# Layer 0 attention's beginning: the first four heads' parts sent ahead, zero fills on ScalarE, other batches' norms placed behind the first scores

## The chip, the cores and the metric

The kernel runs on one core of a Trainium2 chip. The metric is the device time of one launch in microseconds (us); the time before is the median of three runs.

The core's engines have queues of their own, and each works through its queue in order: TensorE (PE, with its weight loads as PEld), VectorE (DVE), ScalarE (ACT), GpSimd (POOL) and SyncE (SP), which here only issues transfers (DMA). An instruction that waits holds everything behind it on its engine.

## The reference, cut to what matters

A decoder of four layers runs on x of shape 4 x 512 x 128 (batches, tokens, width). Each layer is an attention, a cross-attention to a context of 77 rows, and a feed-forward with experts, each added to x. The change is in the first of these twelve parts, and touches the second:

```
x = x + L0_attn(layernorm(x), W_attn, b_attn, W_proj, b_proj, temperature)
x = x + L0_xattn(ctx, ctx, layernorm(x), ...)
```

`L0_attn` has 16 heads of width 8. Its scores are q k^T / sqrt(8) divided by a temperature, with a bias for the distance of two tokens (a slope for each head), and a causal mask; softmax and the product with v follow, then a projection with W_proj. The kernel keeps the accuracy of 32 bits in the scores by splitting q and k into three bf16 parts each and multiplying the parts.

## The kernel before, in words

The program is written for a planner (the Tile framework): Python code emits instructions in one order; the planner puts each on its engine's queue, may move an instruction ahead of earlier ones that are not ready by its own account, and adds the waits. `weave(dense, chain, every)` (L386) interleaves two generators when emitting: after `every` steps of the first it takes one of the second. What the planner makes of it is seen in the trace.

At the start `Net.__init__` fetches x of batch 0, weights, constants and x of batches 1 to 3 (L318, L371), and makes the identity, the ones and the causal mask on GpSimd. `norm(0)` (L491) follows: statistics of four tiles of 128 tokens (L479, L480), a reciprocal square root by Newton steps on 128x4 elements (L465 to L470), scaling on ScalarE (L487), four TensorE transposes into the PSUM tile s, of which there is one (L511), and a copy to xT (L512).

`l0_attn` (L1034) then prepares its tiles. The two tiles `vs` (one batch each, alternating; 128 x 2048 elements) are filled with zeros, and every ninth column of a group of 32 with ones, on GpSimd (L1057, L1058). `project(b)` makes a batch's q and k: two matmuls of xT (L421), q on VectorE (L1089), k on ScalarE (L1090); the parts, by casts on ScalarE (L1094, L1098) and subtractions on VectorE (L432), into `q3` and `k5`; a copy of two parts of `k5` on GpSimd (L1101), so that three consecutive parts can be taken in three rotations. Then the parts are written to DRAM, one transfer for q (L1105) and three for k (L1107), in all for 16 heads at once; last come the values v (L1112, L1113). `load(b, g)` brings the rows of four heads (group g) from DRAM into `qs[g]` and `ks[g]` in six transfers of 96 KB (L1121, L1122), in which a row of the contraction is a partition.

`rounds(first, last)` runs 16 items (4 batches x 4 groups). For item 0, `project(0)`, `load(0, 0)`, the bias row (L1076) and `load(0, 1)` come first. In a round the scores of one item are computed in 11 units (L1132, the mask added by L1135), each followed by a maximum on VectorE (L1139); beside them stand the scores again, transposed and less the maxima, with the exponential, of the item before (L1177 to L1185), whose maxima are sent as rows into `qs` (L1161 to L1165), and the product with v of the item before that (L1199). The next batch's `project` is spread over the round of its predecessor's second group, and each round loads the item two ahead.

At the end, the caller weaves rounds 0 to 6 with a chain: `norm(1)`, `norm(2)`, `norm(3)` and `l0_context`, which projects the 77 context rows of the four batches for the cross-attention (matmuls L421 on tile s, a copy L427, an addition L1315, a copy L429). One step of the chain is emitted after four steps of the rounds.

Of the kernel before, what the change touches and what calls it, by code (L numbers as in the profile page):

```python
# [14 lines left out]
BF16 = mybir.dt.bfloat16  # L15
# [7 lines left out]
P = 128  # L23
B, S, D = 4, 512, 128
NT = B * S // P
TB = S // P
# [12 lines left out]
class Pack:  # L39


    def __init__(self):
        self.parts, self.at, self.n = [], {}, 0
# [246 lines left out]
class Net:  # L290
# [7 lines left out]
    def __init__(self, ctx, tc, packs, dram, feed):  # L298
        self.tc, self.nc = tc, tc.nc
        self.packs, self.dram = packs, dram  # L300
        self.feed, self.loaded = feed, []
        self.stay = {}
        self.turn = 0
        self.last = []
        self.chunks, self.sums = {}, {}
        nc = self.nc
        pool = lambda name, bufs, **kw: ctx.enter_context(tc.tile_pool(name=name, bufs=bufs, **kw))
        self.keep = pool("keep", 1)
        self.wpool = pool("weights", self.SLOTS)
        self.small = pool("small", 4)  # L310
        self.away = pool("away", 1, space=bass.MemoryType.DRAM)

        k = self.keep
        self.x = k.tile([P, NT, D], F32, name="x")
        self.xn = k.tile([P, NT, D], F32, name="xn")
        self.xT = k.tile([P, NT * P], F32, name="xT")
        xin = dram["x"].rearrange("(t p) d -> p t d", p=P)
        fetch = lambda b: nc.sync.dma_start(self.x[:, TB * b : TB * b + TB, :], xin[:, TB * b : TB * b + TB, :])  # L318
        fetch(0)
        self.want(0)  # L320
        self.const = self.load("const", k, "const")
        self.want(1)
        for b in range(1, B):
            fetch(b)
        self.ident = k.tile([P, P], F32, name="ident")
        make_identity(nc, self.ident)
        self.ones = k.tile([P, P], F32, name="ones")
        nc.gpsimd.memset(self.ones, 1.0)
        self.identb = k.tile([P, P], BF16, name="identb")
        nc.vector.tensor_copy(self.identb, self.ident)  # L330

        self.causal = k.tile([P, P], BF16, name="causal")
        nc.gpsimd.memset(self.causal, 0.0)
        nc.gpsimd.affine_select(
            out=self.causal, in_=self.causal, pattern=[[-1, P]], compare_op=ALU.is_ge,
            fill=-BIG, base=0, channel_multiplier=1,
        )
# [3 lines left out]
    def pool(self, name, bufs=1, right=False):  # L341
        return self.tc.tile_pool(
            name=name, bufs=bufs, side="right" if right else "left", reuse_waits="tile"
        )
# [21 lines left out]
    def load(self, name, pool, tag, cols=None):  # L366
        at, n = self.packs[name]
        src = self.dram[name]
        t = pool.tile([P, cols or n], F32, tag=tag, name="w_" + name.replace(".", "_"))
        cast = src.dtype != F32  # L370
        (self.nc.gpsimd if cast else self.nc.sync).dma_start(t[:, :n], src)  # L371
        return Weights(t, at)
# [25 lines left out]
    def turns(self, *chains):  # L398

        chains = [iter(c) for c in chains]  # L400
        while chains:
            for c in list(chains):
                try:
                    yield next(c)
                except StopIteration:
                    chains.remove(c)

    def lagged(self, items, *phases):

        for r in range(len(items) + max(lag for _, lag in phases)):  # L410
            for phase, lag in phases:
                if 0 <= r - lag < len(items):
                    phase(*items[r - lag])
                    yield
# [619 lines left out]
    def l0_attn(self, pool, W, Wo):  # L1034
# [3 lines left out]
        nc, tc = self.nc, self.tc  # L1038
        one = lambda shape, name, dt=F32: pool.tile(shape, dt, name=name, bufs=1)
        K1, K2 = 81, 99  # L1040
        qs = [one([K2, 4, S], f"qs{g}", BF16) for g in range(4)]
        ks = [one([K2, 4, S], f"ks{g}", BF16) for g in range(4)]
# [11 lines left out]
        vs = [one([P, TB, 16, 32], f"v{i}") for i in range(2)]  # L1054
        for v in vs:

            nc.gpsimd.memset(v, 0.0)  # L1057
            nc.gpsimd.memset(v[:, :, :, 8:9], 1.0)  # L1058

        rows = one([48, 16], "own_rows")  # L1060
# [19 lines left out]
        made, ys, stacks = {}, {}, {}  # L1080

        def project(b):

            xb = self.tokens(b)
            pq, pk = self.mm(), self.mm()
            self.dot(pq, (W["wq"], xb))
            self.dot(pk, (W["wk"], xb))
            q, k = (pool.tile([P, S], F32, tag=n, name=n, bufs=1) for n in "qk")
            nc.vector.tensor_scalar(q, pq, W["bq"], sc, ALU.add, ALU.mult)  # L1089
            nc.scalar.activation(k, pk, AF.Identity, bias=W["bk"])  # L1090
            yield
            q3, k5 = pool.tile([P, 3, S], BF16, tag="q3", name="q3"), pool.tile([P, 5, S], BF16, tag="k5", name="k5")
            for a, out in ((q, q3), (k, k5)):
                nc.scalar.copy(out[:, 0], a)  # L1094
                self.tt(a, a, out[:, 0], ALU.subtract)
            yield
            for a, out in ((q, q3), (k, k5)):
                nc.scalar.copy(out[:, 1], a)  # L1098
                self.tt(out[:, 2], a, out[:, 1], ALU.subtract)
            yield  # L1100
            nc.gpsimd.tensor_copy(k5[:, 3:5], k5[:, 0:2])  # L1101
            qd = self.away.tile([16, 24, S], BF16, name=f"q_parts{b}")
            kd = [self.away.tile([16, 24, S], BF16, name=f"k_parts{b}_{c}") for c in range(3)]
            flat = lambda d: d.rearrange("h (d p) t -> (h d) (p t)", p=3)
            nc.sync.dma_start(flat(qd), q3.rearrange("r p t -> r (p t)"))  # L1105
            for c in range(3):
                nc.sync.dma_start(flat(kd[c]), k5[:, c : c + 3].rearrange("r p t -> r (p t)"))  # L1107
            stacks[b] = qd, kd
            yield
            ps = self.mm((P, TB, 16, 8))  # L1110
            for j in range(TB):
                self.dot(ps[:, j].rearrange("p h d -> p (h d)"), (self.tile_of(TB * b + j), W["wv"]))  # L1112
            nc.scalar.copy(vs[b % 2][:, :, :, :8], ps)  # L1113
            yield

        def load(b, g):

            qd, kd = stacks[b]
            for c in range(3):
                r = slice(24 * c, 24 * c + 24)  # L1120
                nc.sync.dma_start(qs[g][r], qd[4 * g : 4 * g + 4].rearrange("h r t -> r h t"))  # L1121
                nc.sync.dma_start(ks[g][r], kd[c][4 * g : 4 * g + 4].rearrange("h r t -> r h t"))  # L1122

        def score_units(b, g):

            m = made[b, g, "m"] = pool.tile([P, TB, 4], F32, tag="m", name="m", bufs=2)

            def unit(i, h0, per):
                n = (i + 1) * P
                ps = self.mm((P, per, n))  # L1130
                for h in range(per):
                    nc.tensor.matmul(  # L1132
                        ps[:, h], lhsT=qs[g][:K1, h0 + h, i * P : n], rhs=ks[g][:K1, h0 + h, :n], start=h == 0, stop=False
                    )
                nc.tensor.matmul(  # L1135
                    ps[:, :, i * P :], lhsT=self.identb, rhs=self.causal.unsqueeze(1).to_broadcast([P, per, P]),
                    start=False, stop=True,
                )
                nc.vector.tensor_reduce(m[:, i, h0 : h0 + per], ps, AX.X, ALU.max, negate=True)  # L1139

            return [
                lambda i=i, h0=h0, per=per: unit(i, h0, per)
                for i, per in ((3, 1), (2, 1), (1, 2), (0, 4)) for h0 in range(0, 4, per)
            ]
# [89 lines left out]
        def rounds(first, last):  # L1234
            n = len(items)
            item = lambda i: items[i] if 0 <= i < n else None
            if first == 0:
                yield from project(0)
                load(0, 0)
                biases()  # L1240
                load(0, 1)
                yield
# [927 lines left out]
def chained(*chains):  # L2170
    for c in chains:
        yield from c
# [10 lines left out]
def build(nc, packs, dram):  # L2183
# [11 lines left out]
    with tile.TileContext(nc) as tc, ExitStack() as ctx:  # L2195
        net = Net(ctx, tc, packs, dram, feed)
# [3 lines left out]
        def open_pool(name, right=False):  # L2200
            pools[name] = ExitStack()
            return pools[name].enter_context(net.pool(name, right=right))
# [10 lines left out]
        s1 = open_pool("s1", right=True)  # L2213
# [3 lines left out]
            pass  # L2217
        rounds = net.l0_attn(a0, *[net.pack(i, feed[i]) for i in range(2)])
        w1 = net.load("s1", s1, "w")
        net.weave(rounds(0, 7), chained(net.norm(1), net.norm(2), net.norm(3), net.l0_context(s1, w1)), 4)  # L2220
        net.want(at["l0a"] + 1)

        def chain1(group):
# [62 lines left out]
        rounds = net.l2_ffn(f2, gv, y, away, passes, where, wants)  # L2286
# [57 lines left out]
        chain = chained(net.norm(3), net.route_dense(3, W5, s5))  # L2344
# [31 lines left out]
```

## Time and profile before

| what | value |
|---|---|
| median of 3 runs | 2305.12 us (2304.5 to 2309.32) |
| the profiled execution's own time | 2308.67 us |
| its span | 2306.8 us |
| TensorE busy | 2164.1 us (94%) |
| VectorE busy | 1600.5 us (69%) |
| ScalarE busy | 1027.8 us (45%) |
| GpSimd busy | 556.6 us (24%) |
| first score matmul (L1132) starts | 33.2 us |
| moved by DMA in the whole span | 204.72 MB |

The span is what the profiler records between the first and the last instruction; the time of an execution is a little longer. Busy time is the time in which an engine executes; weight loads overlap matmuls. In a timeline a line gives start, length, engine, line of the code, operation, output<-input, size and count; in brackets, how long the engine had been idle before and what ended it. A count above one joins neighbouring instructions. "SPq" is SyncE's queue: its lines are transfers being issued, not their landing.

### The profile page before, as it was taken

The numbers are of one execution on the slowest core, as the hardware profiler recorded it, in microseconds if no ns is written. First come the engines' busy times: TensorE is split into PE (matmuls) and PEld (weight loads), VectorE is DVE, ScalarE is ACT, GpSimd is POOL, SyncE is SP. The second block draws the span as 40 slices with busy tenths as digits, with TensorE's granted clock in tenths as the row PEclk, the third lists the DMA queues.
The fourth block names the chain that finished last, engine by engine and source line by source line (L and its number), as shares of the span: only waits on it lengthen the run. The fifth ranks groups of instructions, "written<-read, shape, count | busy, mean of one in ns | idle before, by whom it ended". The sixth has DMA issues, their size and how long they took to land. (4 is left out here: it accounts for less than half of the span.)

```text
span 2306.8 us, 28326 instructions
## 1 busy us (share of the span) xinstructions
PE 2164.1 (94%) x9154; PEld 1142.8 (50%) x9154; DVE 1600.5 (69%) x4027; ACT 1027.8 (45%) x2102; POOL 556.6 (24%) x693
## 2 busy tenths in 40 slices
PE   6999899999999998999999999999999999498878
PEld 3566556554545553444444444444444444465553
DVE  6666576566675779777967696767776765686636
ACT  4555446444325462544444344444444444165432
POOL 1000001000000002333323333333333332335552
PEclk8988899999999999999999999999999999799779
DMA  6321134153453344233333344333333334200022
GB/s 165 99 61 43 45 108 132 51 141 104 110 148 90 90 103 117 59 94 94 92 85 82 87 113 108 103 103 94 103 103 94 82 99 101 92 1 6 1 71 75
DMA packets 81774, 204.72 MB, mean 89 GB/s; under 512 B 18799, under 2 KB 37551, under 8 KB 81371
## 3 DMA queue, kind: packets, MB, share of 16 engines
q1 hardware_dynamic: 78058, 198.99, 32.2%
q0 software_dynamic: 3568, 3.93, 0.6%
q8 instruction: 72, 1.18, 0.2%
q14 instruction: 76, 0.61, 0.1%
HBM read 173.94 MB, written 23.40 MB: 86 GB/s over the span
## 5 line engine op out<-in xcount | busy, mean ns | idle before, releaser
L1756 POOL TENSOR_TENSOR gvx<-gvx 128x512 f32<-128x512 f32 (+1 forms) x256 | 259.8, 1015 | 583.7 <-DVE gvx L432 528.6
L421 PE MATMUL f<-xT,w_l_ffn 128*128 128x512 f32 (+1 forms) x768 | 367.9, 601 | 1.2 <-ACT h L1001 0.7
L1876 ACT ACTIVATE at_e<-mm,at_m 128x512 f32<-128x512 f32 x256 | 172.8, 685 | 215.3 <-DVE at_m L1874 209.6
L421 PE MATMUL mm<-w_l_ffn_qkv,xT 128*128 128x512 f32 x512 | 265.5, 603 | 3.3 <-DVE roped L1727 1.7
L1845 PE MATMUL mm<-og,w_l_ffn_o 128*128 128x512 f32 x512 | 264.6, 600 | 0.0
L432 DVE TENSOR_TENSOR h<-h,f 128x512 f32<-128x512 f32 (+1 forms) x192 | 131.3, 685 | 136.1 <-PE f L421 110.3
L1001 ACT ACTIVATE h<-f 128x512 f32<-128x512 f32 x189 | 112.4, 596 | 249.7 <-PE f L421 217.2
L421 PEld LDWEIGHTS f<-xT,w_l_ffn 128*128 128x128 f32 (+1 forms) x768 | 139.5, 191 | 149.0 <-issue 126.1
L1009 PE MATMUL acc<-h,w_l_ffn 128*128 128x512 f32 x378 | 193.4, 596 | 3.5 <-DVE h L432 2.9
L432 DVE TENSOR_TENSOR og<-mm,c 128x512 f32<-128x512 f32 x256 | 175.8, 688 | 29.0 <-PE mm L1845 27.6
L432 DVE TENSOR_TENSOR gvx<-mm,gv 128x512 f32<-128x512 f32 x256 | 174.3, 683 | 23.6 <-PE mm L421 18.9
L1796 ACT COPY eT<-mm 128x512 f32<-128x512 f32 x256 | 137.5, 595 | 73.3 <-PE mm L1795 73.0
L1874 DVE TENSOR_REDUCE at_m<-mm 128x1 f32<-128x512 f32 x256 | 161.2, 683 | 8.9 <-PE mm L421 7.2
L1795 PEld LDWEIGHTS mm<-ident,at_e 128*128 128x128 f32 x1024 | 120.1, 141 | 67.0 <-issue 49.5
L1845 PEld LDWEIGHTS mm<-og,w_l_ffn_o 128*128 128x128 f32 x512 | 89.4, 191 | 97.0 <-issue 85.3
L1795 PE MATMUL mm<-ident,at_e 128*128 128x128 f32 x1024 | 134.1, 273 | 2.6 <-ACT at_e L1876 2.6
L421 PE MATMUL mm<-roped 64*128 64x512 f32 x512 | 133.4, 623 | 1.5 <-DVE roped L432 1.0
L421 PEld LDWEIGHTS mm<-w_l_ffn_qkv,xT 128*128 128x128 f32 x512 | 86.7, 190 | 91.9 <-issue 69.4
L1139 DVE TENSOR_REDUCE m<-mm 128x1 f32<-128x512 f32 (+3 forms) x176 | 105.3, 637 | 35.5 <-PE mm L1135 34.7
L1812 PE MATMUL mm<-eT,v 128*64 128x512 f32 x512 | 119.5, 599 | 0.0
L1009 PEld LDWEIGHTS acc<-h,w_l_ffn 128*128 128x128 f32 x378 | 70.9, 191 | 92.9 <-issue 66.9
L432 DVE TENSOR_TENSOR h<-h,c 128x512 f32<-128x512 f32 x160 | 111.1, 700 | 3.9 <-DMA c<-l_ffn_w 1.1
(457 smaller groups left out, 3646.3 us busy)
## 6 DMA issues: line engine op xcount, KB each, us to landing
c<-gates SPq DMA_DIRECT2D x256, 256.0 KB
c<-l_ffn_w SPq DMA_DIRECT2D x96, 384.0 KB
w_l_ffn<-in_l_ffn SPq DMA_DIRECT2D x26, 576.0 KB
w_l_ffn_qkv<-in_l_ffn_qkv SPq DMA_DIRECT2D x16, 640.0 KB
w_l_ffn_o<-in_l_ffn_o SPq DMA_DIRECT2D x16, 512.0 KB
rot<-qk SPq DMA_DIRECT2D x128, 64.0 KB
k_parts<-k SPq DMA_DIRECT2D x12, 384.0 KB
qs<-q_parts SPq DMA_DIRECT2D x48, 96.0 KB
```

Source lines behind the costliest of these rows:

```text
L421: self.nc.tensor.matmul(out, lhsT=lhsT, rhs=rhs, start=i == 0, stop=i == len(pairs) - 1)
L432: self.nc.vector.tensor_tensor(out, a, b, op)
L1001: nc.scalar.activation(h, pg, AF.Silu)
L1009: nc.tensor.matmul(acc["t"], lhsT=W["d" + u], rhs=h, start=i == 0, stop=i == n - 1)
L1139: nc.vector.tensor_reduce(m[:, i, h0 : h0 + per], ps, AX.X, ALU.max, negate=True)
L1756: nc.gpsimd.tensor_tensor(x[:, :, :m], x[:, :, :m], x[:, :, m : 2 * m], ALU.add)
L1795: nc.tensor.transpose(p[:, j, :], es[i][hl][:, j * P : j * P + P], self.ident)
L1796: nc.scalar.copy(eT[hl][:, :, i * P : i * P + P], p)
L1812: nc.tensor.matmul(po[64 * hl : 64 * hl + 64, :], lhsT=m["v"][:, j, hl, :], rhs=eT[hl][:, j, :], start=j == 0, stop=j == TB - 1,)
L1845: nc.tensor.matmul(acc, lhsT=W["o"][:, (e - 1) * D : e * D], rhs=hs.pop(e - 1), start=e == 1, stop=e == E)
L1874: nc.vector.tensor_reduce(m, s, AX.X, ALU.max, negate=True)
L1876: nc.scalar.activation(e[:, :n], s, AF.Exp, bias=m, accum_out=den)
```

## The change

Five edits, all in the first stage:

- the zero fills of `vs` move from GpSimd to ScalarE, as a scaled copy of the ones by 0.0;
- the copy of two parts of `k5` moves from GpSimd to VectorE, for every batch;
- batch 0's parts go to DRAM in two sets of four transfers, heads 0 to 3 and then heads 4 to 15, in DRAM tiles of their own; `load(b, g)` finds the tile that holds its group;
- `load(0, 0)` is emitted between these two sets instead of after `project(0)`;
- the chain of norms and context is wrapped in `after_scores`: once a first score matmul has been emitted, every TensorE instruction of the chain is ordered behind it on TensorE's queue (an order of issue, no wait for its end). Instructions of the chain on other engines are not ordered by it.

```diff
+    def after_scores(self, chain):
+
+        while True:
+            with ExitStack() as order:
+                if self.first_score:
+                    order.enter_context(self.tc.issue_after(self.first_score.ins))
+                if next(chain, chain) is chain:
+                    return
+            yield
...
-            nc.gpsimd.memset(v, 0.0)
+            flat = v.rearrange("p j h i -> p (j h i)").rearrange("p (n c) -> p n c", c=P)
+            nc.scalar.mul(flat, self.ones.unsqueeze(1).to_broadcast([P, TB * 16 * 32 // P, P]), 0.0)
             nc.gpsimd.memset(v[:, :, :, 8:9], 1.0)
...
-            nc.gpsimd.tensor_copy(k5[:, 3:5], k5[:, 0:2])
-            qd = self.away.tile([16, 24, S], BF16, name=f"q_parts{b}")
-            kd = [self.away.tile([16, 24, S], BF16, name=f"k_parts{b}_{c}") for c in range(3)]
+            nc.vector.tensor_copy(k5[:, 3:5], k5[:, 0:2])
+
+            parts = ((0, 4), (4, 16)) if b == 0 else ((0, 16),)
             flat = lambda d: d.rearrange("h (d p) t -> (h d) (p t)", p=3)
-            nc.sync.dma_start(flat(qd), q3.rearrange("r p t -> r (p t)"))
-            for c in range(3):
-                nc.sync.dma_start(flat(kd[c]), k5[:, c : c + 3].rearrange("r p t -> r (p t)"))
-            stacks[b] = qd, kd
+            stacks[b] = []
+            for h0, h1 in parts:
+                r = slice(8 * h0, 8 * h1)
+                qd = self.away.tile([h1 - h0, 24, S], BF16, name=f"q_parts{b}_{h0}")
+                kd = [self.away.tile([h1 - h0, 24, S], BF16, name=f"k_parts{b}_{h0}_{c}") for c in range(3)]
+                nc.sync.dma_start(flat(qd), q3[r].rearrange("r p t -> r (p t)"))
+                for c in range(3):
+                    nc.sync.dma_start(flat(kd[c]), k5[r, c : c + 3].rearrange("r p t -> r (p t)"))
+                stacks[b].append((h0, h1, qd, kd))
+                if h0 == 0 and b == 0:
+                    load(0, 0)
...
-            qd, kd = stacks[b]
+            (h0, _, qd, kd), = [part for part in stacks[b] if part[0] <= 4 * g < part[1]]
+            h = slice(4 * g - h0, 4 * g - h0 + 4)
...
-                nc.sync.dma_start(qs[g][r], qd[4 * g : 4 * g + 4].rearrange("h r t -> r h t"))
-                nc.sync.dma_start(ks[g][r], kd[c][4 * g : 4 * g + 4].rearrange("h r t -> r h t"))
+                nc.sync.dma_start(qs[g][r], qd[h].rearrange("h r t -> r h t"))
+                nc.sync.dma_start(ks[g][r], kd[c][h].rearrange("h r t -> r h t"))
...
-                    nc.tensor.matmul(
+                    product = nc.tensor.matmul(
...
+                    self.first_score = self.first_score or product
...
                 yield from project(0)
-                load(0, 0)
                 biases()
...
-        net.weave(rounds(0, 7), chained(net.norm(1), net.norm(2), net.norm(3), net.l0_context(s1, w1)), 4)
+        chain = chained(net.norm(1), net.norm(2), net.norm(3), net.l0_context(s1, w1))
+        net.weave(rounds(0, 7), net.after_scores(chain), 4)
```

More of the change, by code (lines that the diff above doesn't have):

```diff
@@ L302, in __init__ @@
         self.stay = {}
+        self.first_score = None
         self.turn = 0
```

## The prediction

> **What bounds the kernel now.** The page's part 2 first: PE is near 9 tenths in almost every slice, and the first slice (57.7 us each) has 6. TensorE work therefore carries most of the kernel, and a microsecond saved before its dense part should shift all that follows. The chain that ended last covers 5% of the span only and holds nothing of the beginning, so I read the beginning by stage: busy time in chosen stretches (columns: stretch, PE, PEld, DVE, ACT, POOL, granted clock, DMA share, GB/s).
>
> ```profile
> 15.50:20.30 4.80, 3.17 (x18) 2.25 (x17) 4.80 (x24) 4.47 (x9) 0.86 (x1) 1.00 0.55 122
> 20.30:25.30 5.00, 2.90 (x8) 1.27 (x8) 2.67 (x15) 3.94 (x10) 0.86 (x1) 0.54 0.93 351
> 25.30:33.00 7.70, 5.82 (x16) 3.13 (x16) 1.02 (x2) 1.52 (x4) 0.00 (x0) 0.50 0.84 158
> 33.00:40.20 7.20, 7.20 (x33) 4.09 (x33) 6.18 (x12) 0.58 (x1) 0.00 (x0) 0.50 0.28 51
> 40.20:50.30 10.10, 7.19 (x43) 3.55 (x42) 9.48 (x19) 5.52 (x10) 1.04 (x1) 0.95 0.18 46
> ```
>
> Until 20.3 VectorE is full, until 33.0 the DMA, then rounds 0 and 1 keep VectorE at 6.18 of 7.20 and 9.48 of 10.10. TensorE runs at half clock from 21 to 41. Next the timeline, for what holds the first score (L1132):
>
> ```profile
> 2.41 3.54 POOL L1057 MEMSET v<- 128x2048 f32 x2
> 4.95 1.17 DVE L465 TENSOR_SCALAR rs_v<-mv 128x4 f32<-128x4 f32 x1
> ...
> 14.66 0.29 DVE L479 BATCH_NORM_STATS2 st<-x 128x6 f32<-128x128 f32 x1 [0.33 <-DMA x<-in_x]
> 15.42 0.79 DVE L1089 TENSOR_SCALAR q<-mm,w_l_attn_qk,sc 128x512 f32<-128x512 f32 x1
> ...
> 19.68 0.36 SPq L1105 DMA_DIRECT2D q_parts<-q  x1
> 20.28 1.74 SPq L1107 DMA_DIRECT2D k_parts<-k  x3
> 22.11 0.72 SPq L1121 DMA_DIRECT2D qs<-q_parts  x1
> 25.23 0.29 SPq L1122 DMA_DIRECT2D ks<-k_parts  x1
> 29.18 0.29 SPq L1121 DMA_DIRECT2D qs<-q_parts  x1
> 31.43 1.99 PE L421 MATMUL s<-w_s,vT 128*77 128x128 f32 x8 [0.63 <-DVE vT L1315]
> 33.21 0.63 PE L1132 MATMUL mm<-ks,qs 81*128 81x512 bf16 x1
> 46.66 1.04 POOL L1101 COPY k<-k 128x1024 bf16<-128x1024 bf16 x1 [25.50 <-ACT k L1098]
> 46.74 1.50 DVE L432 TENSOR_TENSOR q<-q,q 128x512 bf16<-128x512 f32 x1
> ```
>
> And SyncE's waits from 17 to 34 us (total, times, longest):
>
> ```profile
> SPq L1121 <- DMA ks<-k_parts: 0.3, 1, 0.3
> ```
>
> That wait is the issue at 29.18, held 0.3 us by the sixth load of heads 0 to 3 (issued 25.23). So their rows were in SBUF at about 29.15, and the first score still started at 33.2: TensorE's queue held the transposes of batches 1 to 3 and the context's matmuls in front, the last of them at 31.43. Two things hold it, the transfers until 29.15 and the order on TensorE for 4 us more.
>
> [...] the 4-element operation at 4.95 took 1.17 us beside the fill, 0.15 at 13.25 without; the subtraction at 46.74 took 1.50 us beside GpSimd's copy, 0.67 at 18.98. [...] Here a 3 KB row transfer issued at 43.94 freed TensorE at 45.83, 1.9 us. [...] Here half rate stayed 8.2 us after the first score, although TensorE was full.
>
> **Fills off GpSimd.** Two fills of 1.80 us leave GpSimd. ScalarE gains two scaled copies of 128x2048; its 128x512 copy takes 0.61 us[...]. ScalarE is idle to 8.87 apart from a 1.28 us table load[...]. Batch 0's norm loses about 1.0 + 0.4 + 0.2 = 1.6 us of VectorE stretching. But this does not reach the scores: q at 15.42 stood in VectorE's queue behind batch 3's statistics, which waited for x at 14.66, though its matmul (3.78 us from 11.72, the first half for q) was out by 13.7. From there VectorE is full to 20.2. I take 0 (at least 0; at most 1.6, if the planner reorders). [...]
>
> **The copy k5[3:5] to VectorE.** GpSimd's 1.73 us (19.44 to 21.17) goes; k_parts 1 and 2 waited 0.5 us for it. [...] It runs after k's last part (19.58 + 0.67)[...]; behind it stand only norm operations of batches 2 and 3, needed much later. The fourth write's issue moves from 21.7 to about 21.1. In round 1, full on VectorE, it removes 1.50 - 0.67 = 0.83[...]: 0.4 gained. In round 5 the same (1.53 at 91.21), half of it on the path, 0.2; rounds 9 and 13 I leave at nothing.
>
> **Batch 0 in two parts.** Four writes of 384 KB become four of 96 and four of 288 KB: four more issues of 0.36 us on SyncE, and none on GpSimd's queue. Before, 512 packets of 3072 B moved from 20.8 to 25.0, then 1 KB loads at some 150 GB/s beside those of the next heads. After: small writes issue at 19.68, 20.28, 20.7, 21.1; each lands 2.0 us later (1.9 fixed), the last at 23.1. The six loads, issued 0.4 apart and each behind its write, go from 21.7 to 23.9; the last, 96 KB with free engines, lands in 1.9 + 0.35: 26.2. Behind the waiting loads stand, on SyncE, the four large writes (now at 24 to 25.5, landed about 28.8), the row wp, and heads 4 to 7, landed near 31.3 instead of 30; round 1 needs these at 33, so 1.7 us of cover. On the planner: all of SyncE's transfers up to 58 us stand in program order, so I take the loads ahead of the large writes. First score 33.2 - 26.2 = 7.0 us earlier.
>
> **Norms and context behind the first score.** Nothing is removed: the work on tile s is 9.56 us of TensorE from 17 to 50 us, all at half clock (4.8 at full). Before, it was hidden by the transfers but for the last 4 us. After, it competes. Round 0 at half clock needs 6.0 us of TensorE against 6.14 of VectorE, so a norm put in it costs its 1.63 us; the other 8.0 (4.0 at full clock) meet round 1's idle time, 10.10 - 7.19 = 2.9: 1.1 over. Given back: 2.7, from 1 (later rounds absorb it: 62.4 to 74.6 has 2.7 idle) to 7 (all at half clock, 9.56 less 2.9). Statistics and row scaling are not on TensorE and stay early. Queued behind the transposes are ScalarE's xT copies (0.58), and batch 1's projection in round 1 waits for the first; one bank s makes the chain serial, 14 us before, and only its first link is due in round 1.
>
> Sum: 7.0 - 2.7 + 0.4 + 0.2 = 4.9, and 0.6 as half of what the upstream 1.6 and a later round's idle time may add: 5.5. The profiled execution took 2308.67 around its span of 2306.8, so 2303.2 with a span of 2301.3; the median shown is 3.55 below that execution: 2305.12 - 5.5 = 2299.6.
>
> **Rivals.** (a) The large writes go ahead of the loads on SyncE: data at 29.15 as before, and TensorE's order brings 4.0 only: 4.0 - 2.7 + 0.6 = 1.9, 2303.2. For: all eight writes are ready at once. Against: the program order seen. (b) The moved work comes back in full: give-back 7, gain 0.6, 2304.5. For: rounds 0 and 1 are nearly full; against: 2.9 us idle in round 1. (c) Slower: the clock stays at half through round 1[...]. Then rounds 0 and 1 need 7.2 + 2 x 7.19 + 9.56 = 31.1 us of TensorE from 26.2, ending at 57.3 against 50.3: 7 us slower, 2312. It decides from 17 us of half clock after the first score (8.2 before): 14 of the 31.1 us must run at full clock to end by 50.3. Against: fp32 projections stand in round 1, and the clock rose as soon as they came (40.25 and 41.4).
>
> **How the numbers follow.** 0.2% is 4.6 us, about what a measurement of this kernel can tell from no change. All edits work: 0.70, own range 2295 to 2303, 0.56 of it beyond 4.6. (a) 0.12, (b) 0.08, both within. (c) or something like it in a later round's order: 0.10. So faster 0.56, same 0.34, slower 0.10. Range 2293 to 2308: below it only both upper ends at once (7.0 + 1.6 + 0.6 + a give-back of nothing, with more in later rounds); above it most of (c).
>
> **What would show it.** First score at 25.5 to 27 us, the small writes' loads issued before the large writes; no stretched operations on VectorE before 7 us, yet q still near 15.4; first tile-s transpose of batch 1 after the first score; round 1 ending near 45 to 46; later rounds with the lengths of before. A first score after 29 speaks for (a); idle VectorE in round 0 with the first score early, for (b); half clock past 43, for (c). I am wrong if the order of later stages on any engine changes by more than this, which no view of before can show.

## The result, and the profile after

The changed kernel took 2311.41 us (median of 22 executions, 2301.07 to 2316.91), the kernel before on the same chip 2304.61 (22 executions, 2298.53 to 2315.91). The ratio is 1.0027, 95% interval 1.0016 to 1.0038: slower by 6.2 us, from 3.7 to 8.8. The forecast was 2299.6 with a range of 2293 to 2308, so the sign was wrong and the range missed the time. The profiled execution took 2312.47 us with a span of 2310.4.

First the same stretches of the changed kernel as those shown of before (columns: stretch, PE, PEld, DVE, ACT, POOL, granted clock, DMA share, GB/s):

```profile
15.50:20.30 4.80, 0.57 (x6) 0.23 (x3) 4.80 (x34) 2.52 (x5) 0.00 (x0) 1.00 0.47 133
20.30:25.30 5.00, 0.00 (x0) 0.00 (x0) 4.05 (x23) 4.15 (x11) 0.00 (x0) 0.55 0.54 143
25.30:33.00 7.70, 4.90 (x22) 2.87 (x23) 4.18 (x8) 1.01 (x3) 0.00 (x0) 0.50 0.84 247
33.00:40.20 7.20, 5.20 (x23) 3.05 (x21) 3.27 (x9) 1.76 (x3) 0.00 (x0) 0.74 0.51 101
40.20:50.30 10.10, 7.92 (x36) 4.34 (x36) 5.84 (x10) 4.05 (x8) 0.00 (x0) 0.78 0.01 2
```

TensorE now does nothing while the parts travel to DRAM and back (0.57 and 0.00 us, before 3.17 and 2.90); below, work that runs in this time is said to stand in the transfers' shade. What is new is further down: from 33.0 to 50.3 VectorE is busy for 3.27 and 5.84 us, where it had 6.18 and 9.48. DMA is all but idle in the last row, so no transfer is what VectorE lacks; it lacks scores.

The timeline of the changed kernel up to the first score, for the steps of the forecast:

```profile
2.03 3.71 ACT L1069 ACTIVATE v<-ones 128x2048 f32<-128x2048 f32 x2
4.94 0.17 DVE L476 TENSOR_SCALAR rs_v<-mv 128x4 f32<-128x4 f32 x1
...
14.85 0.29 DVE L490 BATCH_NORM_STATS2 st<-x 128x6 f32<-128x128 f32 x1 [1.09 <-DMA x<-in_x]
16.59 0.80 DVE L1101 TENSOR_SCALAR q<-mm,w_l_attn_qk,sc 128x512 f32<-128x512 f32 x1
...
21.36 0.41 DVE L1113 COPY k<-k 128x1024 bf16<-128x1024 bf16 x1
21.45 1.24 SPq L1124 DMA_DIRECT2D k_parts<-k  x3
22.79 0.34 SPq L1141 DMA_DIRECT2D qs<-q_parts  x1
...
24.86 0.37 SPq L1142 DMA_DIRECT2D ks<-k_parts  x1
25.27 0.36 SPq L1122 DMA_DIRECT2D q_parts<-q  x1
25.67 2.06 SPq L1124 DMA_DIRECT2D k_parts<-k  x3
...
28.10 0.58 PE L1152 MATMUL mm<-ks,qs 81*128 81x512 bf16 x1 [12.02 <-DMA ks<-k_parts]
```

The fills, the copy and the split do what they say: the loads of heads 0 to 3 (22.79 to 24.86) go out ahead of the large writes (25.27), and the first score starts at 28.10 instead of 33.2, held by the load alone. The 5.1 us are real (in the second profile of each kernel, 28.6 against 34.0). TensorE's timeline behind it shows where they went:

```profile
33.17 1.06 PE L522 MATMUL s<-ident,xn 128*128 128x128 f32 x4
34.02 0.58 PE L1152 MATMUL mm<-ks,qs 81*128 81x128 bf16 x4
34.44 0.38 PE L1156 MATMUL mm<-causal,identb 128*128 128x512 bf16 x1
34.90 0.66 PE L522 MATMUL s<-ident,xn 128*128 128x128 f32 x4
36.24 0.66 PE L522 MATMUL s<-ident,xn 128*128 128x128 f32 x4 [0.68 <-ACT xT L523]
37.57 1.17 PE L432 MATMUL s<-w_const,w_s 128*128 128x308 f32 x2 [0.68 <-ACT xT L523]
39.31 1.40 PE L432 MATMUL s<-w_const,w_s 128*128 128x308 f32 x2 [0.57 <-DVE kT L438]
41.34 1.99 PE L432 MATMUL s<-w_s,vT 128*77 128x128 f32 x8 [0.63 <-DVE vT L1335]
43.12 0.63 PE L1152 MATMUL mm<-ks,qs 81*128 81x512 bf16 x1
...
46.29 0.39 PE L1182 MATMUL mm<-identb,d 128*12 128x128 bf16 x4
```

One norm went into round 0 (33.17). The last score of round 0 stands at 34.02, the first of round 1 at 43.12, and between them, from 34.90, stand the norms of batches 2 and 3 and the whole context: 8.2 us, of which 5.9 are matmuls and the rest mostly waits for ScalarE and VectorE to empty the one tile s. TensorE ran them in the order of its queue, so round 1's scores (from 43.12) and the transposes of round 0's maxima (L1182, L1161 before; at 46.29) came behind them. VectorE had long been done with the maxima:

```profile
36.23 0.19 DVE L443 TENSOR_TENSOR d<-d_rest,d 128x16 bf16<-128x16 f32 x1
38.78 0.48 DVE L438 COPY kT<-s 128x308 f32<-128x308 f32 x1 [2.35 <-PE s L432]
40.74 0.54 DVE L1335 TENSOR_SCALAR vT<-s,w_s 128x308 f32<-128x308 f32 x1 [1.49 <-PE s L432]
43.90 1.29 DVE L1160 TENSOR_REDUCE m<-mm 128x1 f32<-128x512 f32 x2 [2.61 <-PE mm L1156]
```

Their last part was ready at 36.4 and transposed at 46.29, 10 us later. In the kernel before these transposes stood at 42.60:

```profile
40.25 2.42 PE L421 MATMUL mm<-xT,w_l_attn_qk 128*128 128x512 f32 x4
42.60 0.39 PE L1161 MATMUL mm<-identb,d 128*12 128x128 bf16 x4
```

So the beginning went from 5.1 us ahead at the first score to 3.7 behind in round 1: 8.8 us given back. I use the time of these transposes below as the mark of round 1.

After this piece TensorE runs the same instructions in the same order in both kernels, but for two transposes of a norm near 161 us (VectorE's order differs a little between 154 and 167 us, too), and in sum it does the same (2162.1 us busy, 2164.1 before). What later rounds add differs from execution to execution, as the stretches of half clock do: from 58.4 to 95.7 us both profiled executions have none, but from 51.5 to 58.3 the changed kernel has one and the kernel before has not. At the last item of layer 0's attention the two profiled executions are 1.0 us apart (256.9 and 257.9). Executions of one kernel scatter over 16 to 17 us, so the cause has to be found from many executions and from the beginning.

### The profile page after: what moved, and what is told of

Read it like the earlier page. It is cut to its first block, busy times and chain, and to the rows that moved or that the text cites. A ratio compares the mean times of both kernels' runs of the same rounds, so it can differ in the third digit from the quotient of the medians.

```text
span 2310.4 us, 28325 instructions
## 1 busy us (share of the span) xinstructions
PE 2162.1 (94%) x9154; PEld 1139.9 (49%) x9154; DVE 1597.7 (69%) x4031; ACT 1032.7 (45%) x2104; POOL 547.5 (24%) x687
## 4 chain that ended last, share of the span: by engine, by line
PE 74%; DVE 15%; issue 4%; POOL 2%; ACT 2%; DMA 2%; SPq 0%; POOLq 0%; ACTq 0%; DVEq 0%
PE mm L432 21%; PE f L432 12%; PE mm L1865 8%; PE s L432 8%; PE acc L1020 6%; PE mm L1832 5%; PE mm L1815 4%; DVE h L443 2%; PE mm L1152 2%; PE mm L1198 1%; PE mm L1220 1%; PE s L522 1%; DVE k_work L443 1%; DVE m L1160 1%; DVE at_m L1894 1%
```

## The experiments

The theories:

- **A**, the order on TensorE: the norms and the context form a serial piece ahead of round 1's scores.
- **B**, the fills on ScalarE or the copy on VectorE delay batch 0's q or the later work.
- **C**, only the half clock falls elsewhere. ("Half clock" is the state in which TensorE is granted half its speed, a granted clock of 0.50, as from 25.3 to 33.0 us above; a half-clock window in the expectations is a stretch of it. The mean granted clock of an execution is on record for each.)
- **D**, work moved out of the transfers' shade costs its time wherever it is put.
- **F** and **G**, for the last two kernels: a shift of the beginning reaches the end in full, or later rounds give most of it back.

The edits are against the changed kernel unless another is named. All results in one table; the ratio is to the kernel before, run beside it on the same chip, and the two marks are from one profiled execution each.

The last two columns come from all executions. The first gives the mean granted clock of the kernel and of the kernel before beside it. Among the executions of one kernel on one chip, a mean clock lower by 0.001 goes with a time longer by 1.8 us (382 executions, all but the first measurement of the changed kernel). The last column is the difference of the mean times, this kernel less the one before, after that slope has been taken out: an estimate of what is left at equal clock, in us, with a 95% interval from the scatter of the executions. The uncertainty of the slope is left out; with 1.5 or 2.1 us in place of 1.8, no row of the column changes its sign.

| kernel | of the chain, ahead of round 1's first scores and behind round 0's | first score | round 1's mark | ratio (95%) | mean clock, this and before | at equal clock |
|---|---|---|---|---|---|---|
| before | nothing | 33.2 | 42.6 | | | |
| before, once more | nothing | 34.0 | 44.7 | | | |
| changed | norms 2, 3, context in full | 28.1 | 46.3 | 1.0027 (1.0016 to 1.0038) | 0.9583, not recorded | |
| changed, once more | the same | 28.6 | 47.6 | 1.0032 (1.0018 to 1.0045) | 0.9525, 0.9553 | +1.9 ± 1.8 |
| fills on GpSimd | the same | 26.5 | 46.3 | 1.0032 (1.002 to 1.0043) | 0.9580, 0.9609 | +2.0 ± 1.0 |
| order alone | norms 2, 3, two steps of the context | 29.1 | 42.8 | 1.002 (1.0008 to 1.0032) | 0.9603, 0.9609 | +3.0 ± 1.3 |
| no split | norms 2, 3, two steps of the context | 29.3 | 46.4 | 1.001 (0.9994 to 1.0026) | 0.9594, 0.9604 | +1.4 ± 1.2 |
| no order | nothing | 33.4 | 41.2 | 1.0012 (1.0 to 1.0025) | 0.9585, 0.9609 | -2.0 ± 1.1 |
| latest score | nothing | 25.6 | 37.7 | 0.9994 (0.9977 to 1.001) | 0.9600, 0.9609 | -2.6 ± 1.2 |
| latest score, once more | nothing | 26.7 | 36.3 | 1.0015 (1.0002 to 1.0028) | 0.9523, 0.9553 | -2.1 ± 1.5 |
| two late | nothing | 27.1 | 39.4 | 1.0004 (0.9989 to 1.002) | 0.9585, 0.9604 | -2.2 ± 1.2 |
| context late | nothing | 27.2 | 38.8 | 0.9992 (0.9973 to 1.0011) | 0.9599, 0.9604 | -3.3 ± 1.5 |
| context late, once more | nothing | 27.5 | 39.3 | 1.0 (0.9986 to 1.0014) | 0.9535, 0.9553 | -3.4 ± 1.1 |
| context late, third | nothing | 25.3 | 36.2 | 0.9984 (0.9972 to 0.9996) | 0.9557, 0.9552 | -2.9 ± 1.2 |
| late copies | nothing | 38.3 | 46.7 | 1.0052 (1.0032 to 1.0072) | 0.9508, 0.9552 | +3.0 ± 2.0 |

**No order.** The chain is woven in without `after_scores`; fills, copy and split stay.

```diff
-        net.weave(rounds(0, 7), net.after_scores(chain), 4)
+        net.weave(rounds(0, 7), chain, 4)
```

> The changed kernel less its order on TensorE (the chain of norms and context is woven in plainly); fills, copy and split stay. Theory A (the chain, now one serial piece ahead of round 1's scores, eats what the early first score gains): the chain returns ahead of the first scores, which start near 34 us, round 1's transposes of the maxima (46.3 us in the changed kernel, 42.6 before) come near 43, and the time is that of before within 2 us. Theory B (fills and copy delay q and with it everything): the first score is even later, near 35, and the time is 3 us or more above before. Theory C (nothing in the beginning, only how the half-clock windows fall later): no difference to the changed kernel.

2304.34 us against 2302.91, ratio 1.0012 (1.0 to 1.0025). The norms and the context are back in front of the first score, which starts at 33.36:

```profile
31.57 1.99 PE L432 MATMUL s<-w_s,vT 128*77 128x128 f32 x8 [0.63 <-DVE vT L1335]
33.36 0.63 PE L1152 MATMUL mm<-ks,qs 81*128 81x512 bf16 x1
...
41.19 0.39 PE L1182 MATMUL mm<-identb,d 128*12 128x128 bf16 x4 [1.14 <-DVE d L443]
```

By the median most of the loss is gone. The first score is as late as before, with the context in front of it. The interval overlaps with that of the changed kernel, so the ratio alone does not settle it; it also leaves open a loss of up to 0.0025 from the other four edits. At equal clock this kernel is 4.0 us (plus or minus 1.3) faster than the one with the fills on GpSimd beside it, which has the order and, but for the fills, the same edits.

**Order alone.** The kernel before with `after_scores` around the chain, and nothing else of the change (the method itself and the line that notes the first score come with it).

```diff
+        chain = chained(net.norm(1), net.norm(2), net.norm(3), net.l0_context(s1, w1))
+        net.weave(rounds(0, 7), net.after_scores(chain), 4)
-        net.weave(rounds(0, 7), chained(net.norm(1), net.norm(2), net.norm(3), net.l0_context(s1, w1)), 4)
```

> The kernel before plus only the order on TensorE. Theory A: first score at 29.2 us instead of 33.2, then batches 2 and 3's norms and two of the context's three steps ahead of round 1's scores; round 1's transposes of the maxima come at 44 to 46 instead of 42.6, and the time is 2 to 5 us above before. Theory B: 3 to 4 us under before, since q is not delayed here. Theory C: as before.

2307.66 us, ratio 1.002 (1.0008 to 1.0032): this edit by itself makes the kernel before slower by 4.8 us. Its TensorE timeline between the rounds:

```profile
34.93 0.39 PE L1143 MATMUL mm<-ks,qs 81*128 81x128 bf16 x4
...
35.77 0.66 PE L522 MATMUL s<-ident,xn 128*128 128x128 f32 x4 [0.23 <-ACT xT L523]
37.10 0.66 PE L522 MATMUL s<-ident,xn 128*128 128x128 f32 x4 [0.68 <-ACT xT L523]
38.43 0.79 PE L432 MATMUL s<-w_const,w_s 128*128 128x308 f32 x2 [0.68 <-ACT xT L523]
39.79 0.79 PE L432 MATMUL s<-w_const,w_s 128*128 128x308 f32 x2 [0.57 <-DVE kT L438]
40.41 0.38 PE L1143 MATMUL mm<-ks,qs 81*128 81x512 bf16 x1
```

The same piece, 5.4 us from the end of round 0's scores to round 1's first, although the granted clock was 1.00 throughout: its matmuls then take 0.66 to 0.79 us, and the waits for the tile s remain. One forecast failed: round 1's mark was expected at 44 to 46 us and stood at 42.8, about as in the kernel before. That execution, 2298.98 us, was the fastest of the 22 and had no half clock between 34.9 and 209 us, while the kernel before had it until 41.2; the loss of this kernel shows in the medians and at equal clock (3.0 us), not in its mark.

**Latest score.** Each TensorE instruction of the chain is ordered behind the latest score that was emitted, not behind the first of all. The order in which the chain was emitted is thus kept among the rounds.

```diff
-                    self.first_score = self.first_score or product
+                    self.first_score = product
```

> The changed kernel with each TensorE instruction of the chain ordered behind the last score emitted so far, not the first one: batch 1's norm stays in round 0, batch 2's goes to round 2, batch 3's to round 3, the context to round 4. Theory A: no serial piece ahead of round 1, round 1's transposes of the maxima near 39 us instead of 46.3, 7 to 9 us less than the changed kernel and 1 to 4 less than before. Theory B: as the changed kernel, at most 2 us less. Theory C: no difference.

2301.42 us, ratio 0.9994 (0.9977 to 1.001), against 1.0032 (1.002 to 1.0043) of the kernel with the fills back on GpSimd, beside it on the same chip. The intervals are apart, and at equal clock the difference of the two is 4.5 us. Only one norm is ahead of round 1:

```profile
30.63 1.06 PE L522 MATMUL s<-ident,xn 128*128 128x128 f32 x4
31.48 0.63 PE L1152 MATMUL mm<-ks,qs 81*128 81x128 bf16 x4
31.91 0.63 PE L1156 MATMUL mm<-causal,identb 128*128 128x512 bf16 x1
33.12 0.58 PE L1152 MATMUL mm<-ks,qs 81*128 81x512 bf16 x1 [0.58 <-DMA ks<-k_parts]
...
37.73 0.39 PE L1182 MATMUL mm<-identb,d 128*12 128x128 bf16 x4
...
48.77 0.60 PE L522 MATMUL s<-ident,xn 128*128 128x128 f32 x4
```

Norm 2 comes at 48.77, norm 3 at 63.27, the context from 67.99 to 76.0. In the changed kernel the planner had placed them as early as the order allowed, directly behind round 0, though they are emitted during the later rounds.

**Fills on GpSimd.** The two zero fills go back.

```diff
-            nc.scalar.mul(flat, self.ones.unsqueeze(1).to_broadcast([P, TB * 16 * 32 // P, P]), 0.0)
+            nc.gpsimd.memset(v, 0.0)
```

> The changed kernel with its zero fills back on GpSimd; the order on TensorE is the same as in the changed kernel. Theory A: q on VectorE moves by 1 us or less (16.6 us in the changed kernel, 15.4 before), the serial piece stays, the time is that of the changed kernel within 2 us. Theory B: q is back at 15.4, first score near 27, the time 3 us or more under the changed kernel. Theory C: no difference.

2310.71 us, ratio 1.0032. VectorE is stretched again (1.28 us for the 4-element operation at 4.86, against 0.17 with the fills on ScalarE), yet q starts at 13.91 and the first score at 26.47, both earlier than with the fills on ScalarE (q moved by 2.7 us, where at most 1 was expected; the x transfers scatter by as much, see below). The piece on TensorE stands from 33.27 to 41.58, and the ratio is that of the changed kernel within its interval. So the place of the fills does not show in the time; B falls for them. The copy was not moved alone; "latest score" has it on VectorE as well and is not slower than before on this chip.

**Context late.** As "latest score", but the norms are free and only the context is ordered.

```diff
-        chain = chained(net.norm(1), net.norm(2), net.norm(3), net.l0_context(s1, w1))
-        net.weave(rounds(0, 7), net.after_scores(chain), 4)
+        chain = chained(net.norm(1), net.norm(2), net.norm(3), net.after_scores(net.l0_context(s1, w1)))
+        net.weave(rounds(0, 7), chain, 4)
```

> The changed kernel, but only the context's three steps are ordered, each behind the last score emitted so far (they come to rounds 4 and 5); the norms of batches 1 to 3 are woven plainly, so their transposes stand ahead of the first scores, while the parts are still on their way. Theory A with its addition (what is moved behind the scores comes back, since rounds 2 and later have little idle TensorE time): first score at 27 to 28.5 us, round 1's transposes of the maxima near 39, 2 to 5 us less than before, 1 to 3 less than e3_last_score. Against it (moved work is hidden in rounds 2 to 4 and something else limits e3_last_score): no better than e3_last_score.

2300.97 us against 2303.07, ratio 0.9992 (0.9973 to 1.0011). The norms stand in the transfers' shade again:

```profile
20.05 1.48 PE L522 MATMUL s<-ident,xn 128*128 128x128 f32 x4 [3.74 <-ACT xn L498]
22.60 1.63 PE L522 MATMUL s<-ident,xn 128*128 128x128 f32 x4 [1.06 <-ACT xn L498]
24.91 1.63 PE L522 MATMUL s<-ident,xn 128*128 128x128 f32 x4 [0.68 <-ACT xT L523]
27.19 0.59 PE L1152 MATMUL mm<-ks,qs 81*128 81x512 bf16 x1 [0.65 <-DMA ks<-k_parts]
...
38.76 0.39 PE L1182 MATMUL mm<-identb,d 128*12 128x128 bf16 x4
```

The last transposes end at 26.54, 0.65 us before the load lands, so the norms cost the first score nothing; the context runs from 68.73 to 76.7. That it would be 1 to 3 us faster than "latest score" can't be seen in these intervals.

**Two late.** As "context late", with norm 3 ordered behind the latest score too.

```diff
-        chain = chained(net.norm(1), net.norm(2), net.norm(3), net.l0_context(s1, w1))
-        net.weave(rounds(0, 7), net.after_scores(chain), 4)
+        late = net.after_scores(chained(net.norm(3), net.l0_context(s1, w1)))
+        net.weave(rounds(0, 7), chained(net.norm(1), net.norm(2), late), 4)
```

> As e5_context_late, and batch 3's norm is ordered late too (round 3). First score at 25.5 to 28 us, as soon as its rows are there; 2.6 us of TensorE work at half clock less ahead of the scores than in e5_context_late and 0.9 more in round 3. Theory A with its addition: 2 to 5 us less than before, within 1 us of e5_context_late. Against it: as e3_last_score.

2306.31 us, ratio 1.0004 (0.9989 to 1.002); it can't be told from "context late", and the gain of 2 to 5 us that was expected is not seen.

**No split.** Batch 0's parts go in one set again; all else as changed.

```diff
-            parts = ((0, 4), (4, 16)) if b == 0 else ((0, 16),)
+            parts = ((0, 16),)
```

> The changed kernel with batch 0's parts written in one set of four transfers and the loads of heads 0 to 3 behind them; order, fills and copy stay. The planner then leaves only batches 2 and 3's norms and two steps of the context ahead of round 1's scores, the third step comes later. Theory A: first score at 28 to 30 us, the time 1 to 3 us under the changed kernel and 3 to 5 above before. If the split itself helps under this order: slower than the changed kernel by 1 us or more.

2306.78 us, ratio 1.001 (0.9994 to 1.0026). The first score comes at 29.32, as the forecast gave for the data without a split (29.15), and q had started at 15.55. From q to the first score it is 13.8 us, with the split 11.5 to 12.6 in the profiled executions: the split is worth 1.2 to 2.3 us there. Round 1's mark is that of the changed kernel (46.4), the ratio lower, within its uncertainty; whether the split brings or costs time under this order stays open.

**Before, once more.** A second profile of the kernel before.

> The kernel before, profiled once more. [...] this one shows another length (13.7 us from 21 on, as in most other profiles) and round 1's transposes of the maxima near 41 instead of 42.6; first score at 33 us in both.

Round 1's mark is at 44.7 instead of 42.6: half clock lasted 23.9 us from 20.9, instead of 20.5. The forecast was the other way, 13.7 us and a mark near 41. This is the size of what an unchanged kernel does at this mark. By it and by the second profile of the changed kernel (47.6), the changed kernel is 1.6 to 5.0 us behind in round 1, and C stays as an explanation of single executions. As the only cause it falls: the order behind the first score is slower in all five kernels that have it, in four of them by more than the uncertainty, and the four whose clocks can be compared stay slower at equal clock. But it has its share in the medians, see "What follows".

**The three once more,** on another chip, on which the kernel before took 2324.18 us.

> The norms free, each context step behind the latest score, in more rounds. Theory A (the serial block ahead of round 1 is the loss, and the earlier first score is worth something once the block is gone): faster than the kernel before by 2 to 5 us, ratio 0.998 to 0.999 with an interval that leaves 1 out; round 1's shift transposes at 37.5 to 41 us, where the kernel before has them at 42.6 to 44.7. Theory D (work of TensorE that leaves the transfers' shade costs its time wherever it is put): ratio 0.9995 to 1.001.

> Every piece of the chain behind the latest score, in more rounds. Theory A: faster than the kernel before by 1 to 4 us, ratio 0.9985 to 0.9995, first score at 25.5 to 28 us, round 1's shift transposes at 37 to 40 us. Theory D: ratio 0.9995 to 1.001. If the norms in the transfers' shade are worth anything, it is slower than the kernel with the norms free by about 1 us or more.

> The changed kernel once more beside these two. Theory A: ratio 1.002 to 1.004, round 1's shift transposes at 45 to 47 us, with the block of norms 2 and 3 and of the context between round 0's and round 1's scores again.

The changed kernel was slower again (1.0032, 1.0018 to 1.0045), "context late" was as before (1.0, 0.9986 to 1.0014), and these intervals are apart. "Latest score" was at 1.0015 (1.0002 to 1.0028), slower than before although its round 1 began earliest of the three (36.3). My expectation of a gain failed for both, and by the ratios D is not refuted. Both ran at a lower clock than the kernel before, though (0.9535 and 0.9523 against 0.9553); at equal clock they are 3.4 and 2.1 us faster, as in their other runs, which speaks against D. Norms in the transfers' shade look better than norms in later rounds by 0.0015, 3.5 us, but these two intervals overlap.

**Late copies.** To see whether a shift of the beginning reaches the end at all: "context late" with batch 0's copy made 25 times over, beside the same kernel without that.

```diff
-            nc.vector.tensor_copy(k5[:, 3:5], k5[:, 0:2])
+            for _ in range(25 if b == 0 else 1):
+                nc.vector.tensor_copy(k5[:, 3:5], k5[:, 0:2])
```

> The kernel with the norms free and the context behind the latest score, in which VectorE makes batch 0's copy of two parts of k5 25 times over, so 24 x 0.41 = 9.8 us before the second and third k parts can be written; nothing else differs. First score near 37 instead of 27 us, round 1's shift transposes near 48 to 49. Theory F (a shift of the beginning reaches the end in full): ratio to the kernel before 0.004 above that of the same kernel without the copies. Theory G (later rounds give most of a shift back, so that a later beginning costs and an earlier one gains little): 0.002 above it or less, and the last round's shift transposes less than 5 us later.

> The same kernel without the repeated copies, beside it. Theory F: its first score some 5 us and its round 1 some 4 us earlier than in the kernel before should leave it 4 us faster, ratio 0.998, unless the moved work costs the same again later. Theory G: ratio 0.999 to 1.001.

With the copies, TensorE's timeline is this (the two marks):

```profile
38.32 0.58 PE L1153 MATMUL mm<-ks,qs 81*128 81x512 bf16 x1 [8.77 <-DMA k_parts<-k]
...
46.65 0.39 PE L1183 MATMUL mm<-identb,d 128*12 128x128 bf16 x4
```

Without them:

```profile
25.28 0.58 PE L1152 MATMUL mm<-ks,qs 81*128 81x512 bf16 x1 [0.92 <-DMA ks<-k_parts]
...
36.16 0.39 PE L1182 MATMUL mm<-identb,d 128*12 128x128 bf16 x4
```

The first score is 13.0 us later, round 1 10.5, and the ratios differ by 0.0068 (1.0052 and 0.9984; with the two half widths combined, 0.0020 and 0.0012, 0.0045 to 0.0091): 10 to 21 us. The last round's transposes come at 263.4 us against 242.1, 21.3 us later. By the bounds that were set (0.004 against 0.002 or less, and under 5 us in the last round) F holds and G falls: a delay of the beginning is seen at the end. That it arrives "in full" is not shown, since the kernel with the copies ran at a mean clock of 0.9508 against 0.9557: at equal clock 5.8 us (plus or minus 2.0) are left, about half of the shift in round 1. Why it ran at the lower clock is open. "Context late" itself was faster here, 0.9984 (0.9972 to 0.9996). Its three ratios, weighted by the inverse squares of their half widths (0.0019, 0.0014, 0.0012), give 0.9991, plus or minus 0.0008: about 2 us faster than the kernel before, between nothing and 4.

**What follows.** A holds. The order alone costs 4.8 us by the medians and 3.0 at equal clock. At equal clock "fills on GpSimd" is 4.0 and 4.5 us slower than "no order" and "latest score" beside it, and "changed, once more" 4.0 and 5.3 us slower than "latest score" and "context late" beside it: with the serial piece ahead of round 1 the kernel is slower, without it faster, on both chips. B fell for the fills.

C is not the whole cause, but a good part of the loss goes with the clock. "Fills on GpSimd" and "changed, once more" had a mean clock lower than the kernel before by 0.0029 and 0.0028, outside the scatter; at 1.8 us per 0.001 this is 5 of their 7 us, and 2 us are left at equal clock. "No order" had a lower clock as well (0.0024), "order alone" hardly (0.0006), so the lower clock isn't tied to the order. What lowers it, and where in the 2.3 ms, no run shows.

"Context late" is 2.9 to 3.4 us faster than the kernel before at equal clock in all three measurements, about 2 by the ratios. It leads in round 1 by 3 to 8.5 us (36.2 to 39.3 against 42.6 to 44.7). That less is seen at the end may in part be the context, which now takes 0.73 + 0.68 + 1.05 = 2.5 us of TensorE in a later round instead of the transfers' shade. This last reading is argued, not shown.

## Why the prediction was wrong

**First score 7.0 us earlier.** Right in mechanism, 5.1 in size in the profiled execution. From q's start to the first score the working gave 26.2 - 15.42 = 10.8 us; it was 11.5, and 11.6 to 12.6 in the other kernels with the same beginning: 0.7 or more too little for the small writes and their loads. (The 1.9 us of the working are of one 3 KB transfer in the trace of before, issued by SyncE, as all these are; that they hold for larger ones, and the 0.35 us added for 96 KB, were my estimates, with no measurement behind them.) The other 1.2 are q itself (16.59), behind statistics of batch 2 whose x landed at 14.85 instead of 12.78. In other kernels with the same beginning q started anywhere from 13.2 to 16.9, so this is scatter of the x transfers. First scores of 25.3 to 28.6 us are seen.

**Fills at nothing.** Right. They took 1.86 us each (how long they would take on ScalarE was my estimate, with no measurement behind it), the stretching went (0.17 instead of 1.17), and with them back on GpSimd the ratio was the same within its interval.

**The copy.** It took 0.41 us on VectorE, and the subtraction beside it in round 1 took 0.68 us (1.50 before). The 0.4 us that were to be gained in round 1, and the 0.2 in round 5, rested on my estimate of the copy's length, with no measurement behind it. VectorE was not the bound there: it was idle for 4.3 of the 10.1 us. No gain is seen; the copy was not moved alone.

**SyncE's order.** Right: loads ahead of the large writes. Rival (a) did not occur. What was overlooked is small: the large writes put heads 4 to 7 so late that, where nothing else holds round 1, its first score waits for them, 0.58 us at 33.12 in "latest score", 1.1 in "context late, once more".

**Norms and context behind the first score: given back 2.7.** This is the step that failed. It distributed the 9.56 us of TensorE by capacity: one norm in round 0, and "the other 8.0 (4.0 at full clock) meet round 1's idle time". It did not ask at which place of TensorE's queue the work would stand. The order names the first score alone, so the planner was free to put the rest anywhere behind it, and it put norms 2 and 3 and the context in one piece ahead of all of round 1's scores. There, from 34.90 to 43.12, they met no idle time; they made it, on VectorE (idle for 5.8 of the 8.2 us), and round 1's idle time was still to come after them. The working itself said that one bank s makes the chain serial, 14 us before, and did not price what stands behind a serial piece: 8.2 us, waits included, not 4.0 of matmul. Given back were 8.8 us at the mark of round 1, above the upper bound of 7, which counted no waits. Rival (b), a give-back in full, was right in that the work comes back and too small for the same reason; the idle VectorE that it named as its sign came ahead of round 1, not in round 0.

This step is not the whole distance. The forecast was 5.5 us faster. At equal clock the kernel is about 2 us slower ("changed, once more" and, but for the fills, "fills on GpSimd"), which is 7.5 us from the forecast; some 5 us more go with the lower clock of the executions, a term that the sum put at nothing.

**Rival (c)** had the sign and nearly the time (2312). Its sign, half clock past 43 us, was seen, but not its course: half clock ended at 34.4 us and came back from 37.8 to 44.7, so that the clock of 33.0 to 40.2 was 0.74 (before 0.50), that of 40.2 to 50.3 0.78 (before 0.95), about even over both. The kernel with the order alone had the full clock, 1.00, from 35.0 to 50.3 us in its profiled execution and the piece all the same, of 5.4 us: half clock is not needed for it. Why the clock should stay at half was my assumption, which no trace of before shows. Nor is it shown that round 1's projections end half clock: in the second profile of the kernel before they came at 41.07, and it ended at 44.8. The lower clock found in the executions is a mean over the whole of each, and (c) reckoned with rounds 0 and 1 only. (The working reads 8.2 us of half clock behind the first score of the kernel before; it ended at 41.2, after 8.0.)

**How the numbers followed.** The slower side was given 0.10 and one mechanism. The prediction had the fact from which the right one follows, a wait of scores behind the chain on TensorE, as the gain of 4 us before the first score, and did not ask whether the same wait would come back one round later.

## What to carry to other kernels

An edge that says "not before X" also sets free what it is put on: a planner may place it directly behind X, in front of the next critical piece. To spread work over later rounds, tie each piece to its own round, and leave in the transfers' shade what ends before the data arrive. Price a moved serial chain by its length with its round trips on the engine that it blocks (8.2 us here), not by its busy time against idle time of the same stretch (4.0 less 2.9 in the forecast). And read the mean clock beside the time of every execution: of the 0.3% here, 5 of 7 us are by estimate the clock's.

## What the runs showed of the hardware

From 21 us on half clock lasted 20.5 and 23.9 us in two executions of the kernel before, 13.7 in the changed one, 17.1 in "latest score": within 0.1 us, six, seven, four and five times the 3.41 us of the short stretch that the kernel before has at 119.7. TensorE's busy time in the trace, taken in pieces of this length, does not tell when the clock changes. In the changed kernel TensorE was busy for 2.91 of 3.41 us from 27.6 and for all of the next 3.41, and then had the full clock (34.4). In the kernel before, half clock went on through 3.41 us in which TensorE was busy throughout and ended after another 3.41 of the kind (34.4 to 41.2), in its second profile after a third (34.6 to 44.8). Nor does an equal share bring half clock back: after 1.98 of 3.41 us busy from 34.4 it came in the changed kernel, after some 1.95 from 34.9 in "order alone" it did not. What counts for it stays open. Where the stretches fall differs between executions of one kernel, whose times lie up to 17 us apart in the 22 of the kernel before.

The same x transfers landed at different times in different executions: the third batch's statistics, which wait for them, began at 11.3 to 14.9 us. This moves the first score as much as the edits on GpSimd and SyncE. On two of the chips the kernel before took 2323 to 2324 us, on others 2303 to 2305, 0.9% less; only ratios from one chip can be compared. Its mean clock was 0.955 on the two and 0.960 to 0.961 on two of the others; at 1.8 us per 0.001 this would be about half of the 20 us, an estimate.
